# A two-layer FFT-attention kernel: the first element loads its rows in fours and in a fixed order

## The chip, the cores and the metric

The kernel runs on one core of one Trainium2 chip. A core has five engines that run their own instruction queues in order: PE (matrix products), DVE (vector), ACT (activations), POOL and SP. SP, ACT and POOL also issue DMA transfers, which sixteen DMA engines of the core carry out. An instruction starts when the semaphores it waits for have reached their counts. The metric is the device time of one execution in microseconds; the times shown are medians of several executions.

## The reference

The input x is 8 x 256 x 96 x 96 in fp32 (element, channel, row h, column w). Two layers are applied, each on a group-normalised copy and added to x. Cut to what matters here:

```
def _L0_conv_ref(x, w1, b1, w2, b2, w3, b3, w_out, temperature):
    q_f = jnp.fft.fft2(pconv(x, w1, b1), axes=(-2, -1))
    k_f = jnp.fft.fft2(pconv(x, w2, b2), axes=(-2, -1))
    v_f = jnp.fft.fft2(pconv(x, w3, b3), axes=(-2, -1))
    ...
    attn = jnp.einsum('bhcn,bhdn->bhcd', q_f, k_f) * temperature[None].astype(q_f.dtype)
    attn = jax.lax.complex(jax.nn.softmax(jnp.real(attn), axis=-1), jax.nn.softmax(jnp.imag(attn), axis=-1))
    out = jnp.einsum('bhcd,bhdn->bhcn', attn, v_f)
    out = jnp.abs(jnp.fft.ifft2(out, axes=(-2, -1)))
    out = out.reshape(b, c, h, w)
    return pconv(out, w_out)
```

The result is x + L0(gn(x)), and to that is added L1 of its group norm, a linear attention with softplus features; the change doesn't touch L1.

The kernel never forms q_f and k_f. Their products over all frequencies follow from the channel covariance of x with itself and with x mirrored in both axes, so layer 0 begins with sums over pairs (row h from the front, row h from the back, columns reversed).

## The kernel before

Elements are handled one after another, b = 0 to 7, and two SBUF arenas of 128 partitions x 2 planes x 9232 fp32 change roles: `x_of(b)` and `y_of(b)`. For each element there are these stages.

**Pair sums** (`pair_sums`, L335). Twelve blocks u of four row pairs each, and one block for the middle row (u = 12). Rows are loaded by `load_grouped(b, v)` (L136): for v = 0 to 5 it fetches 8 rows f from the front and their 8 mirror rows g from the back, two rows per partition: partition 32a + i holds rows 2(4v + a) and the next, of channels i, i + 32 and so on. Each of the four blocks a has one transfer for f (L152) and one for g (L154), on SP, 32 partitions x 8 runs of 768 bytes, 192 KB. They go to `staged` (plane v % 2). `turn_blocks(u)` (L350) turns 32 x 32 blocks on DVE (L369) from `staged` into `turned`, f into plane 0 and g into plane 1. After the second block of a v, SP writes `turned` to DRAM (`xtd`, L372, 1536 KB), then the next group is loaded. `pair(u)` (L376) forms the sum f + g on POOL (L391) and the difference on DVE (L392) in a ring of five tiles, and `products` puts 24 matmul passes per block on PE (L343), in three steps q.

**Rotation** (`rotate`, L599). 49 steps, each eight matmul passes with a piece of a rotation table R: L647 multiplies rows read back from `xtd` (`fetch`, L633, into seven slots) with R (`load_r`, L608, from the DRAM tensor `rx`), and DVE and ACT move the product to the y arena (L653, L654). R is made at the start by `tables` (L252): a small table is written to DRAM (L266), read back in overlapping form (L270, 1764 KB in runs of 384 bytes) and written out as `rx` (L279, L280). Then follow small loads of weights on ACT (`load_small`).

**Attention** (`attention`), woven with the remaining rotation steps, then **images** (z and po products, L710, L718) and **layer 1**. In images of element b the rows of b + 1 are loaded, and its pair sums run beside images and layer 1. Only element 0 has its pair sums and its rotation alone.

The order on each engine is the order in which the program is written within `manual_schedule` (L1015). For element 0 a loop over the yields of `pair_sums(0)` adds one part of `tables` per turn from the fifth on, a `fetch` every second turn past 20, and a rotation step per turn past 26. The first loads, `gavg` and `gmat` are issued above, outside of `manual_schedule`. Transfers of SP and ACT share eight completion semaphores; before one is used again, its last transfer must have landed.

Of the kernel before, what the change touches and what calls it, by code (L numbers as in the profile page):

```python
# [57 lines left out]
P = 128  # L58
# [4 lines left out]
TR = 4  # L63
# [10 lines left out]
def two_layer_kernel(ctx: ExitStack, tc: tile.TileContext, x, w1t, b1, w2t, b2, w3, b3, wot, temp,  # L74
# [32 lines left out]
    def x_of(b):  # L107
        return arenas[b % 2]
# [15 lines left out]

    SG = NB8 * 2 * W
    TO = 2 * SG + 4

    def staged(b, v, at=0):

        return x_of(b)[:, v % 2, at * SG:at * SG + SG + at]  # L130

    def turned(b):

        return [x_of(b)[:, c, TO:TO + 2 * NQ * C].rearrange("p (q r n) -> p q r n", q=NQ, r=2) for c in range(2)]

    def load_grouped(b, v):  # L136

        xs = x[b].rearrange("(c i) h w -> i c h w", i=32)
        if 2 * v == NG:
            m = H // 2  # L140
            f, g = (staged(b, v, i)[:, 0:C].rearrange("p (c w) -> p c w", c=NB8) for i in range(2))
# [7 lines left out]
        f, g = (staged(b, v, i)[:, 0:SG].rearrange("p (c w) -> p c w", c=NB8) for i in range(2))  # L149
        for a in range(G):  # L150
            h, s = 2 * (G * v + a), slice(32 * a, 32 * a + 32)
            nc.sync.dma_start(out=f[s], in_=xs[:, :, h:h + 2].rearrange("p c r w -> p c (r w)"))  # L152
            if h:
                nc.sync.dma_start(out=g[s], in_=xs[:, :, H - h - 1:H - h + 1].rearrange("p c r w -> p c (r w)"))  # L154
            else:
                nc.sync.dma_start(out=g[s, :, 0:W], in_=xs[:, :, H - 1])
                nc.sync.dma_start(out=g[s, :, W:2 * W], in_=xs[:, :, 0])

    setup = y_of(0)[:, 0, :]
    t0 = setup[0:H, 0:6 * W]  # L160
    nc.scalar.dma_start(out=t0[:, 0:2 * W], in_=tmat[0, :, W:3 * W])
    for v in range(2):
        load_grouped(0, v)


    ident = const.tile([P, P], F32, name="ident")
    make_identity(nc, ident)
# [21 lines left out]
    nc.scalar.dma_start(out=gavg_sb, in_=gavg)  # L189
    gri = setup[:, 6 * W:6 * W + 2 * P]  # L190
    nc.scalar.dma_start(out=gri, in_=gmat)

    pw = const.tile([P, 1], F32, name="pw")
    nc.vector.memset(pw, 1.0)
# [49 lines left out]
    rt = dram.tile([H, 2 * W], F32, name="rt")  # L244
    NP = NG
    RW = TR * (W + 2) + P - W
    rx = dram.tile([NP + 1, W, RW], F32, name="rx")
# [4 lines left out]
    def tables():  # L252

        pcs = ps_tile("pcs")
        for c in range(2):
            nc.tensor.matmul(pcs[0:H, c:c + 1], lhsT=csn[0:1, c, :], rhs=ones[0:1, 0:1], start=True, stop=True)
        cs = t0[:, 5 * W:5 * W + 2]
        nc.vector.tensor_copy(cs, pcs[0:H, 0:2])
        r0 = t0[:, 2 * W:3 * W]
        nc.vector.tensor_scalar_mul(t0[:, 0:W], t0[:, 0:W], cs[:, 0:1])  # L260
        nc.vector.scalar_tensor_tensor(r0, in0=t0[:, W:2 * W], scalar=cs[:, 1:2], in1=t0[:, 0:W], op0=ALU.mult, op1=ALU.add)
        for i in range(2):
            o = (3 + i) * W
# [3 lines left out]
        big = y_of(0)[0:W, 1, 0:(N + 1) * (W + 2) + P - W]  # L267
        rows = big[:, 0:(N + 1) * (W + 2)].rearrange("p (r w) -> p r w", r=N + 1)
        v = rt[0:N + 1, 1:]
        nc.scalar.dma_start(out=rows[:, :, 1:W + 1], in_=bass.AP(v.tensor, v.offset, [[1, W], [2 * W, N + 1], [1, W]]))  # L270
        nc.scalar.copy(rows[:, :, 0:1], csn[0:W, 2, 0:N + 1].unsqueeze(2))
        nc.scalar.mul(rows[:, :, W + 1:W + 2], csn[0:W, 2, 0:N + 1].unsqueeze(2), -1.0)
        nc.scalar.copy(big[:, (N + 1) * (W + 2):], csn[0:W, 2, 0:P - W])
        yield
        for q in range(NQ):
            s = slice(32 * q, 32 * q + 32)
            v = big[s, 0:NP * TR * (W + 2)]
            src = bass.AP(v.tensor, v.offset, [list(v.ap[0]), [TR * (W + 2), NP], [1, RW]])
            nc.scalar.dma_start(out=rx[0:NP].rearrange("i (j q) w -> q j i w", q=NQ)[q], in_=src)  # L279
# [12 lines left out]
        yield from load_small()  # L292
# [42 lines left out]
    def pair_sums(b):  # L335
# [12 lines left out]
        wrap = two.tile([P, 2 * NB8], F32, tag="wrap", name=f"wrap_{b}")  # L348

        def turn_blocks(u):  # L350

            v, r = divmod(u, 2)
            t = turned(b)
            if u == NG:
                f, g = (staged(b, v, i)[0:W, 0:C].rearrange("p (c w) -> p c w", c=NB8) for i in range(2))
# [5 lines left out]
            f = staged(b, v, 0).rearrange("p (c r w) -> p c r w", c=NB8, r=2)  # L361
            if r == 0:
                g = staged(b, v, 1)
                nc.vector.tensor_copy(wrap, g[:, 0:SG:W])
                nc.vector.tensor_copy(g[:, W:SG + 1:W], wrap)
            o = SG + (1 - r) * W + 1
            g = x_of(b)[:, v % 2, o:o + SG].rearrange("p (c n) -> p c n", c=NB8)[:, :, W - 1::-1]
            for i, src in enumerate((f[:, :, r], g)):
                nc.vector.transpose(out=t[i][:, :, r].rearrange("p q (c i) -> p q c i", c=NB8),  # L369
                                    in_=src.rearrange("p c (q w) -> p q c w", q=NQ))  # L370
            if r:
                nc.sync.dma_start(out=xtd[:, v].rearrange("c p m -> p c m"), in_=x_of(b)[:, :, TO:TO + 2 * NQ * C])  # L372
                if v + 2 <= NG // 2:
                    load_grouped(b, v + 2)

        def pair(u):  # L376

            eo = ring_tile(f"eo_{b}_{u}").rearrange("p (q c n) -> p q c n", q=NQ, c=2)
            nq, np_ = (NQ, P) if u < NG else (1, W)
            ft, gt = (t[0:np_, 0:nq, u % 2] for t in turned(b))  # L380
            e, o = (eo[0:np_, 0:nq, c, 1:C + 1] for c in range(2))
            nc.gpsimd.memset(eo[0:np_, 0:nq, :, 0:CB:CB - 1], 1.0 if u < NG else R2)  # L382
            if u == 0:
# [215 lines left out]
    def rotate(b):  # L599
# [5 lines left out]
        def load_r(i):  # L605
            tm = tm_tile(f"tm_{b}_{i}")
            o = (TR if i < NP else 1) * (W + 2) + P - W
            nc.sync.dma_start(out=tm[:, 0:o], in_=rx[i][:, 0:o])  # L608
            return tm

        order = [(c, h, h // TR) for h in range(0, N, 2) for c in range(2)] + [(0, N, NP)]
        area = x_of(b)
        slots = [area[0:W, k, o + 4 * C * i:o + 4 * C * (i + 1)].rearrange("p (c m) -> p c m", c=2)
                 for k, o, n in ((0, LO, 3), (1, LO, 3), (0, LO + 12 * C, 1)) for i in range(n)]
        assert LO + 16 * C <= AW and LO + 12 * C <= LO + NS * CH + 2 * CH
        xts, tms = {}, {}
        at_ = [0]
# [1 line left out]
        def fetch():  # L619
# [36 lines left out]
        def steps():  # L656

            for i in range(len(order)):
                while at_[0] < min(i // 2 + len(slots) - 1, len(order) // 2 + 1):
                    fetch()  # L660
                step(i)
                if i >= 24 and i % 8 == 0 and i // 8 < 6:
                    load_x(b, i // 8 - 3)
                yield

        return fetch, steps()

# [345 lines left out]
    sums = pair_sums(0)  # L1013
    E = mybir.EngineType
    with tc.manual_schedule(engines={E.PE, E.DVE, E.Pool, E.SP, E.Activation}):  # L1015
        parts = tables()
        next(parts)
        fetch, turns = rotate(0)
        for i, _ in enumerate(sums):
            if i > 3:  # L1020
                next(parts, None)
            if i > 20 and i % 2 == 0:
                fetch()
            if i > 26:
                next(turns)
        finish(mix(0, attention(0), turns))
        for b in range(B):
# [60 lines left out]
```

## Time and profile before

| | |
|---|---|
| median of 3 runs | 2663.21 us (2656.18 to 2666.2) |
| time of the profiled execution | 2650.85 us |
| its span (first to last instruction) | 2649.0 us |
| PE busy | 2509.3 us (95%) |
| DVE, ACT, POOL busy | 1789.0, 1155.9, 865.6 us |
| first product of the pair sums (PE L343) | at 16.05 us |
| first rotation step (PE L647) | at 97.11 us |
| last product of the pair sums of element 0 | at 126.46 us, 1.48 us long |
| first z product (PE L710) | at 180.31 us |
| DMA moved | 413.27 MB, mean 156 GB/s |

Busy times are sums over all instructions of an engine. The timeline gives start and length in us; "idle before" names what ended the wait. SPq, ACTq and POOLq are the engines' issue of transfers. DMA share is the mean busy share of the sixteen DMA engines, over 1 where packets overlap.

### The profile page before, as it was taken

To read this page: it belongs to the slowest core of one execution; us is meant where nothing else is said; L and a number is where in the kernel's file an instruction comes from. 1 tells how busy PE (TensorE), PEld (TensorE's weight loads), DVE (VectorE), ACT (ScalarE), POOL (GpSimd) and SP (SyncE) were. 2 spreads that over 40 slices of the span, in tenths; PEclk is the share of its full clock that TensorE was granted. 3 is DMA by queue.
4 is the path that set the end of the run, shared out by engine and by line. 5 is a ranking of instruction groups with operands and counts; after the bars stand their busy time and mean duration, and the time that the engine had idled before them with its cause. 6 is when DMAs were issued, how large, how long until landed. Compare 5 with 4: busy or idle time off the path is not lost. (4 is left out here: it accounts for less than half of the span.)

```text
span 2649.0 us, 41157 instructions
## 1 busy us (share of the span) xinstructions
PE 2509.3 (95%) x15580; PEld 1730.2 (65%) x15580; DVE 1789.0 (68%) x3449; ACT 1155.9 (44%) x1985; POOL 865.6 (33%) x817
## 2 busy tenths in 40 slices
PE   3799999999999999999999999999999999999987
PEld 3775666757677576766668566685666757667544
DVE  3457866577756777568675686757866678766766
ACT  0035353453634526344353544435354353534554
POOL 2213514136042451324422343223523135141311
PEclk8899999999999999999999999999999999999999
DMA  9872628637195461935629264492636826286003
GB/s 210 238 216 60 166 71 270 205 67 189 40 313 161 106 173 57 315 120 143 153 90 305 80 167 129 159 316 42 166 89 230 245 60 179 58 289 210 1 7 144
DMA packets 282797, 413.27 MB, mean 156 GB/s; under 512 B 40772, under 2 KB 208872, under 8 KB 282600
## 3 DMA queue, kind: packets, MB, share of 16 engines
q1 hardware_dynamic: 274304, 406.16, 53.2%
q10 hardware_dynamic: 8296, 4.49, 0.8%
q8 instruction: 123, 2.02, 0.3%
q14 instruction: 74, 0.61, 0.1%
HBM read 256.72 MB, written 153.86 MB: 155 GB/s over the span
## 5 line engine op out<-in xcount | busy, mean ns | idle before, releaser
L710 PE MATMUL z<-arena,mz 128*128 128x384 f32 (+1 forms) x2304 | 593.4, 491 | 0.0
L718 PE MATMUL po<-e,wo 128*128 128x384 f32 x1536 | 527.6, 487 | 1.7 <-ACT e L755 1.7
L754 POOL TENSOR_TENSOR e<-e 128x768 f32<-128x768 f32 x192 | 348.4, 1815 | 552.7 <-ACT e L753 529.3
L343 PE MATMUL acc<-eo 128*128 128x257 f32 (+2 forms) x2368 | 437.1, 336 | 50.0 <-POOL eo L382 23.0
L343 PEld LDWEIGHTS acc<-eo 128*128 128x128 f32 (+1 forms) x2368 | 383.8, 194 | 143.9 <-issue 42.4
L710 PEld LDWEIGHTS z<-arena,mz 128*128 128x128 f32 (+1 forms) x2304 | 310.5, 164 | 236.0 <-issue 51.9
L718 PEld LDWEIGHTS po<-e,wo 128*128 128x128 f32 x1536 | 290.0, 190 | 204.7 <-ACT e L755 7.2
L749 DVE TENSOR_TENSOR e<-z,xT 128x768 f32<-128x768 f32 x384 | 361.9, 950 | 75.4 <-PE z L710 74.9
L647 PEld LDWEIGHTS y<-tm,arena 96*128 96x128 f32 x3072 | 365.9, 195 | 52.9 <-issue 18.9
L647 PE MATMUL y<-tm,arena 96*128 96x128 f32 x3072 | 385.7, 281 | 15.3 <-DMA arena<-xtd 6.4
L753 ACT ACTIVATE e<-e 128x1536 f32<-128x1536 f32 x192 | 284.5, 1482 | 195.2 <-DVE e L749 193.3
L391 POOL TENSOR_TENSOR eo<-arena 128x768 f32<-128x768 f32 x88 | 184.5, 2096 | 536.3 <-DVE arena L369 473.2
L720 DVE TENSOR_TENSOR arena<-arena,po 128x384 f32<-128x384 f32 x384 | 209.9, 553 | 190.0 <-PE po L718 190.0
L755 ACT ACTIVATE e<-e 128x768 f32<-128x768 f32 x192 | 162.0, 844 | 367.1 <-POOL e L754 363.2
L986 POOL TENSOR_TENSOR arena<-arena,po 128x384 f32<-128x384 f32 x180 | 179.1, 1014 | 224.0 <-ACT po L985 224.0
L369 DVE STREAM_TRANSPOSE arena<-arena 128x768 f32<-128x768 f32 x192 | 175.7, 953 | 32.5 <-DMA xtd<-arena 23.0
L299 DVE BATCH_NORM_STATS2 st<-arena 128x6 f32<-128x384 f32 x384 | 194.4, 548 | 0.0
L654 ACT COPY ys<-y 128x4 f32<-128x4 f32 (+1 forms) x200 | 32.4, 162 | 363.8 <-DVE arena L653 363.7
L878 PE MATMUL xT<-ident,arena 128*128 128x128 f32 x1152 | 148.4, 277 | 10.0 <-ACT xT L881 9.6
L878 PEld LDWEIGHTS xT<-ident,arena 128*128 128x128 f32 x1152 | 127.2, 142 | 32.0 <-issue 13.6
L985 ACT COPY po<-o 128x384 f32<-128x384 f32 x180 | 79.0, 485 | 157.4 <-PE o L977 152.4
L653 DVE COPY arena<-y 128x384 f32<-128x384 f32 (+1 forms) x200 | 109.1, 546 | 40.8 <-PE y L647 38.6
(225 smaller groups left out, 2493.1 us busy)
## 6 DMA issues: line engine op xcount, KB each, us to landing
xtd<-arena SPq DMA_DIRECT2D x48, 1536.0 KB
arena<-xtd SPq DMA_DIRECT2D x192, 384.0 KB
arena<-in_x_dram SPq DMA_DIRECT2D x96, 768.0 KB
out_dram<-arena SPq DMA_DIRECT2D x192, 384.0 KB
arena<-in_x_dram SPq DMA_DIRECT2D x376, 192.0 KB
tm<-rx SPq DMA_DIRECT2D x96, 159.0 KB
wl<-in_w1t_dram SPq DMA_DIRECT2D x8, 256.0 KB
wl<-in_w2t_dram SPq DMA_DIRECT2D x8, 256.0 KB
```

Source lines behind the costliest of these rows:

```text
L299: nc.vector.bn_stats(out=st[:, k, c, :], in_=x_of(b)[:, k, c * CH:(c + 1) * CH])
L343: nc.tensor.matmul(acc[c][:, m * (C + 1):m * (C + 1) + C + 1 - m * P], lhsT=eo[0:np_, q, c, 1 + m * P:1 + (m + 1) * P], rhs=eo[0:np_, q, c ...
L391: nc.gpsimd.tensor_add(e, ft, gt)
L647: nc.tensor.matmul(pu[:, o:o + P], lhsT=xt[:, s, k * P:(k + 1) * P], rhs=tm[:, n:n + P], start=True, stop=True)
L710: nc.tensor.matmul(out[:, 0:CH].rearrange("p (h q) -> p h q", q=PR), lhsT=columns(mz, k, c, j), rhs=yz[:, k, f, :, o:o + PR], start=(k == ...
L718: nc.tensor.matmul(po[:, 0:CH], lhsT=wo[:, k, m * P:(m + 1) * P], rhs=e[:, k, :], start=(k == 0), stop=(k == KC - 1))
L720: nc.vector.tensor_add(x[:, m, n], x[:, m, n], po[:, 0:CH])
L749: nc.vector.tensor_add(e[:, 2 * c:2 * c + 2, :].rearrange("p t (q h) -> p t q h", h=H), pz[:, 0:CH].rearrange("p (h q) -> p q h", h=H).uns ...
L753: nc.scalar.activation(e, e, AF.Square)
L754: nc.gpsimd.tensor_add(e[:, 0:2, :], e[:, 0:2, :], e[:, 2:4, :])
L878: nc.tensor.transpose(pt[:, j * C + k * P:j * C + (k + 1) * P], x[:, k, o:o + P], ident)
L986: nc.gpsimd.tensor_add(x[:, m, r], x[:, m, r], t)
```

## The change

Only element 0 and the layout of R in DRAM change.

Rows of element 0 are loaded four to a partition: groups v = 0, 2, 4 of 16 front rows and 16 mirror rows, at 3072 fp32 per half and partition. Groups 0 and 2 lie in the planes of `x_of(0)`, group 4 and the middle row in the y arena. The front half has one transfer per channel group c, eight per group on SP, over 128 partitions, with runs of 1536 bytes; the mirror half stays at one transfer per block of 32 partitions and is issued by ACT. All three groups are issued at the start, inside `manual_schedule`, in program order, with `gavg` and `gmat` behind them on ACT. `turned` gets two places, by v % 2. The writes to `xtd` are issued by POOL. The order of rows in `xtd` changes, and with it the read in `fetch`. R's parts of `tables` come in turns 3 and 9 and from 10 on, `rx` has one long row per partition, rotation steps begin at turn 29 instead of 27, fetches at 18 instead of 22, there are eight slots, and the third `load_x` comes after the steps.

```diff
+    S4 = 2 * SG
+    T4 = 2 * S4 + 4
+    def part_of(b, v, o, n):
+        if b:
+            return x_of(b)[:, v % 2, o:o + n]
+        if 2 * v == NG:
+            return y_of(b)[:, 1, H // 2 * W + H // 4 * HB + o:H // 2 * W + H // 4 * HB + o + n]
+        V = v // 2
+        return x_of(b)[:, V, o:o + n] if V < 2 else y_of(b)[:, 0, 10 * W + o:10 * W + o + n]
+    def turned(b, v):
+        o = TO if b else T4 + v % 2 * 2 * NQ * C
+        return x_of(b)[:, :, o:o + 2 * NQ * C]
...
+        n = 2 if b else 4
+        sg = NB8 * n * W
         for a in range(G):
-            h, s = 2 * (G * v + a), slice(32 * a, 32 * a + 32)
-            nc.sync.dma_start(out=f[s], in_=xs[:, :, h:h + 2].rearrange("p c r w -> p c (r w)"))
+            h, s = 2 * G * v + n * a, slice(32 * a, 32 * a + 32)
+            if b:
+                nc.sync.dma_start(out=f[s], in_=xs[:, :, h:h + n].rearrange("p c r w -> p c (r w)"))
+            else:
+                for c in (2 * a, 2 * a + 1):
+                    z = x[b, 32 * c:32 * c + 32]
+                    nc.sync.dma_start(out=f[:, c], in_=bass.AP(z.tensor, z.offset + 8 * v * W, [[n * W, G], [HW, 32], [1, n * W]]))
+            queue = nc.sync if b else nc.scalar
             if h:
-                nc.sync.dma_start(out=g[s], in_=xs[:, :, H - h - 1:H - h + 1].rearrange("p c r w -> p c (r w)"))
+                queue.dma_start(out=g[s], in_=xs[:, :, H - h - n + 1:H - h + 1].rearrange("p c r w -> p c (r w)"))
...
-    nc.scalar.dma_start(out=t0[:, 0:2 * W], in_=tmat[0, :, W:3 * W])
-    for v in range(2):
-        load_grouped(0, v)
...
-        for q in range(NQ):
-            s = slice(32 * q, 32 * q + 32)
-            v = big[s, 0:NP * TR * (W + 2)]
-            src = bass.AP(v.tensor, v.offset, [list(v.ap[0]), [TR * (W + 2), NP], [1, RW]])
-            nc.scalar.dma_start(out=rx[0:NP].rearrange("i (j q) w -> q j i w", q=NQ)[q], in_=src)
-        nc.scalar.dma_start(out=rx[NP][:, 0:P + 2], in_=big[:, N * (W + 2):N * (W + 2) + P + 2])
+            nc.scalar.dma_start(out=rx.rearrange("(j q) w -> q j w", q=NQ)[q], in_=big[32 * q:32 * q + 32])
+        nc.scalar.dma_start(out=rxm, in_=big[:, N * (W + 2):N * (W + 2) + P + 2])
...
-            if r:
-                nc.sync.dma_start(out=xtd[:, v].rearrange("c p m -> p c m"), in_=x_of(b)[:, :, TO:TO + 2 * NQ * C])
-                if v + 2 <= NG // 2:
+            if u % 2:
+                (nc.sync if b else nc.gpsimd).dma_start(out=xtd[:, v].rearrange("c p m -> p c m"), in_=turned(b, v))
+                if b and v + 2 <= NG // 2 or v + 2 == NG // 2:
                     load_grouped(b, v + 2)
...
-                v, a = divmod(i, G)
+                v, a = divmod(i, G) if b else (i // 8 * 2 + i % 2, i % 8 // 2)
...
     with tc.manual_schedule(engines={E.PE, E.DVE, E.Pool, E.SP, E.Activation}):
+        nc.scalar.dma_start(out=t0[:, 0:2 * W], in_=tmat[0, :, W:3 * W])
+        for v in (0, 2, 4):
+            load_grouped(0, v)
+        nc.scalar.dma_start(out=gavg_sb, in_=gavg)
+        nc.scalar.dma_start(out=gri, in_=gmat)
         parts = tables()
         next(parts)
         fetch, turns = rotate(0)
         for i, _ in enumerate(sums):
-            if i > 3:
+            if i in (3, 9) or i > 9:
                 next(parts, None)
-            if i > 20 and i % 2 == 0:
+            if i > 17 and i % 2 == 0:
                 fetch()
-            if i > 26:
+            if i > 28:
                 next(turns)
```

More of the change, by code (lines that the diff above doesn't have):

```diff
@@ L126, in two_layer_kernel, with blocks_of, middle @@
     TO = 2 * SG + 4
[L128 to L134, printed above, removed]
+    S4 = 2 * SG
+    T4 = 2 * S4 + 4
+    assert T4 + 4 * NQ * C <= AW and NG == 12
+    def part_of(b, v, o, n):
[8 more added lines that the diff above has]
+        return x_of(b)[:, :, o:o + 2 * NQ * C]
+    def blocks_of(b, v):
+        return [turned(b, v)[:, c].rearrange("p (q r n) -> p q r n", q=NQ, r=2) for c in range(2)]
+    def middle(b):
+        return [part_of(b, NG // 2, i * (C + 4), C).rearrange("p (c w) -> p c w", c=NB8) for i in range(2)]
     def load_grouped(b, v):
@@ L140, in load_grouped @@
             m = H // 2
-            f, g = (staged(b, v, i)[:, 0:C].rearrange("p (c w) -> p c w", c=NB8) for i in range(2))
+            f, g = middle(b)
             for q in range(NQ):
@@ L148, in load_grouped @@
             return
-        f, g = (staged(b, v, i)[:, 0:SG].rearrange("p (c w) -> p c w", c=NB8) for i in range(2))
+        n = 2 if b else 4
+        sg = NB8 * n * W
+        f, g = (part_of(b, v, i * sg, sg).rearrange("p (c w) -> p c w", c=NB8) for i in range(2))
         for a in range(G):
-            h, s = 2 * (G * v + a), slice(32 * a, 32 * a + 32)
-            nc.sync.dma_start(out=f[s], in_=xs[:, :, h:h + 2].rearrange("p c r w -> p c (r w)"))
+            h, s = 2 * G * v + n * a, slice(32 * a, 32 * a + 32)
[6 more added lines that the diff above has]
+            queue = nc.sync if b else nc.scalar
             if h:
-                nc.sync.dma_start(out=g[s], in_=xs[:, :, H - h - 1:H - h + 1].rearrange("p c r w -> p c (r w)"))
+                queue.dma_start(out=g[s], in_=xs[:, :, H - h - n + 1:H - h + 1].rearrange("p c r w -> p c (r w)"))
             else:
-                nc.sync.dma_start(out=g[s, :, 0:W], in_=xs[:, :, H - 1])
-                nc.sync.dma_start(out=g[s, :, W:2 * W], in_=xs[:, :, 0])
+                queue.dma_start(out=g[s, :, 0:(n - 1) * W], in_=xs[:, :, H - n + 1:H].rearrange("p c r w -> p c (r w)"))
+                queue.dma_start(out=g[s, :, (n - 1) * W:n * W], in_=xs[:, :, 0])
     setup = y_of(0)[:, 0, :]
     t0 = setup[0:H, 0:6 * W]
-    nc.scalar.dma_start(out=t0[:, 0:2 * W], in_=tmat[0, :, W:3 * W])
-    for v in range(2):
-        load_grouped(0, v)
     ident = const.tile([P, P], F32, name="ident")
@@ L188, in two_layer_kernel @@
     gavg_sb = const.tile([P, P], F32, name="gavg_sb")
-    nc.scalar.dma_start(out=gavg_sb, in_=gavg)
     gri = setup[:, 6 * W:6 * W + 2 * P]
-    nc.scalar.dma_start(out=gri, in_=gmat)
     pw = const.tile([P, 1], F32, name="pw")
@@ L246, in two_layer_kernel @@
     RW = TR * (W + 2) + P - W
-    rx = dram.tile([NP + 1, W, RW], F32, name="rx")
+    RL = (N + 1) * (W + 2) + P - W
+    rx = dram.tile([W, RL], F32, name="rx")
+    rxm = dram.tile([W, P + 2], F32, name="rxm")
     xtd = dram.tile([2, NG // 2, P, 2 * NQ * C], F32, name="xtd")
@@ L266, in tables @@
         nc.scalar.dma_start(out=rt, in_=t0[:, 3 * W:5 * W])
-        big = y_of(0)[0:W, 1, 0:(N + 1) * (W + 2) + P - W]
+        yield
+        big = y_of(0)[0:W, 1, 0:RL]
         rows = big[:, 0:(N + 1) * (W + 2)].rearrange("p (r w) -> p r w", r=N + 1)
@@ L346, in products @@
                                      skip_group_check=True)
-        wrap = two.tile([P, 2 * NB8], F32, tag="wrap", name=f"wrap_{b}")
+        n = 2 if b else 4
+        sg = NB8 * n * W
+        wrap = two.tile([P, n * NB8], F32, tag=f"wrap{n}", name=f"wrap_{b}")
         def turn_blocks(u):
-            v, r = divmod(u, 2)
-            t = turned(b)
+            v, r = u // 2, u % n
+            t = blocks_of(b, v)
             if u == NG:
-                f, g = (staged(b, v, i)[0:W, 0:C].rearrange("p (c w) -> p c w", c=NB8) for i in range(2))
+                f, g = (m[0:W] for m in middle(b))
                 nc.vector.tensor_copy(g[0:32, :, 31:32], f[0:32, :, 0:1])
@@ L360, in turn_blocks @@
                 return
-            f = staged(b, v, 0).rearrange("p (c r w) -> p c r w", c=NB8, r=2)
+            f = part_of(b, v, 0, sg).rearrange("p (c r w) -> p c r w", c=NB8, r=n)
             if r == 0:
[L363 to L367, printed above, removed]
+                nc.vector.tensor_copy(wrap, part_of(b, v, sg, sg)[:, ::W])
+                nc.vector.tensor_copy(part_of(b, v, sg + W, sg - W + 1)[:, ::W], wrap)
+            g = part_of(b, v, sg + (n - 1 - r) * W + 1, sg).rearrange("p (c n) -> p c n", c=NB8)[:, :, W - 1::-1]
             for i, src in enumerate((f[:, :, r], g)):
-                nc.vector.transpose(out=t[i][:, :, r].rearrange("p q (c i) -> p q c i", c=NB8),
+                nc.vector.transpose(out=t[i][:, :, u % 2].rearrange("p q (c i) -> p q c i", c=NB8),
                                     in_=src.rearrange("p c (q w) -> p q c w", q=NQ))
-            if r:
-                nc.sync.dma_start(out=xtd[:, v].rearrange("c p m -> p c m"), in_=x_of(b)[:, :, TO:TO + 2 * NQ * C])
-                if v + 2 <= NG // 2:
+            if u % 2:
+                (nc.sync if b else nc.gpsimd).dma_start(out=xtd[:, v].rearrange("c p m -> p c m"), in_=turned(b, v))
+                if b and v + 2 <= NG // 2 or v + 2 == NG // 2:
                     load_grouped(b, v + 2)
@@ L379, in pair @@
             nq, np_ = (NQ, P) if u < NG else (1, W)
-            ft, gt = (t[0:np_, 0:nq, u % 2] for t in turned(b))
+            ft, gt = (t[0:np_, 0:nq, u % 2] for t in blocks_of(b, u // 2))
             e, o = (eo[0:np_, 0:nq, c, 1:C + 1] for c in range(2))
@@ L607, in load_r @@
             o = (TR if i < NP else 1) * (W + 2) + P - W
-            nc.sync.dma_start(out=tm[:, 0:o], in_=rx[i][:, 0:o])
+            nc.sync.dma_start(out=tm[:, 0:o], in_=rx[:, i * TR * (W + 2):i * TR * (W + 2) + o] if i < NP else rxm)
             return tm
@@ L612, in rotate @@
         area = x_of(b)
+        places = ((0, LO, 3), (1, LO, 3), (0, LO + 12 * C, 1)) if b else ((0, T4 - 16 * C, 4), (1, T4 - 16 * C, 4))
         slots = [area[0:W, k, o + 4 * C * i:o + 4 * C * (i + 1)].rearrange("p (c m) -> p c m", c=2)
-                 for k, o, n in ((0, LO, 3), (1, LO, 3), (0, LO + 12 * C, 1)) for i in range(n)]
+                 for k, o, n in places for i in range(n)]
         assert LO + 16 * C <= AW and LO + 12 * C <= LO + NS * CH + 2 * CH
@@ L661, in steps @@
                 step(i)
-                if i >= 24 and i % 8 == 0 and i // 8 < 6:
+                if i >= 24 and i % 8 == 0 and i // 8 < 6 and (b or i < 40):
                     load_x(b, i // 8 - 3)
                 yield
+            if b == 0:
+                load_x(b, 2)
         return fetch, steps()
```

## The prediction

> **What bounds the kernel now.** I read the page's busy times first, then stretches of 20 us, PE's own timeline of the first 130 us, the waits there, and last the moves around one write to `xtd`.
>
> ```profile
> PE 2509.3 (95%) x15580; PEld 1730.2 (65%) x15580; DVE 1789.0 (68%) x3449; ACT 1155.9 (44%) x1985; POOL 865.6 (33%) x817
> PE   3799999999999999999999999999999999999987
> DMA  9872628637195461935629264492636826286003
> ```
>
> PE is the bound of the whole, except in the first slices, the only ones the change touches. What element 0 gains or loses before its images stage moves everything behind it by as much, since from there on PE is full.
>
> Stretches of 20 us; columns are length, busy PE, PEld, DVE, ACT, POOL with counts, granted clock, DMA share, GB/s:
>
> ```profile
> 0.00:20.00 20.00, 4.75 (x16) 4.14 (x17) 9.77 (x39) 2.05 (x5) 4.24 (x62) 1.00 1.02 191
> 60.00:80.00 20.00, 10.84 (x52) 9.53 (x53) 9.10 (x12) 0.00 (x0) 8.59 (x7) 0.76 0.97 215
> 140.00:160.00 20.00, 20.00 (x146) 17.76 (x146) 10.60 (x25) 6.05 (x18) 2.05 (x4) 1.00 1.00 271
> ```
>
> PE is half idle up to 110 us and full from 120 on. Its own timeline, in start and length:
>
> ```profile
> 16.05 10.49 PE L343 MATMUL acc<-eo 128*128 128x257 f32 x48 [11.65 <-DVE eo L388]
> 36.73 10.40 PE L343 MATMUL acc<-eo 128*128 128x257 f32 x48 [10.20 <-POOL eo L391]
> 62.26 9.60 PE L343 MATMUL acc<-eo 128*128 128x257 f32 x48 [15.12 <-POOL eo L382]
> 78.76 9.88 PE L343 MATMUL acc<-eo 128*128 128x257 f32 x48 [6.90 <-POOL eo L382]
> 126.46 1.48 PE L343 MATMUL acc<-eo 96*128 96x257 f32 x8
> ```
>
> The rows x48 are two blocks u each; between them it waits for POOL's sums, 10 to 15 us a time. The last product ends at 126.46 + 1.48 = 127.9 us. That is the mark I carry over.
>
> Waits up to 130 us (total, times, longest), and the timeline around one write:
>
> ```profile
> POOL eo L391 <- DVE arena L369: 81.3, 10, 20.6
> DVE wrap L364 <- DMA arena<-in_x_dram: 20.9, 5, 6.0
> DVE arena L369 <- DMA xtd<-arena: 20.4, 4, 7.4
> ```
>
> ```profile
> 78.82 0.38 SPq L372 DMA_DIRECT2D xtd<-arena  x1
> 85.00 0.31 SPq L152 DMA_DIRECT2D arena<-in_x_dram  x1
> 85.01 1.84 DVE L369 STREAM_TRANSPOSE arena<-arena 128x768 f32<-128x768 f32 x2 [3.12 <-DMA xtd<-arena]
> ```
>
> POOL waits for DVE's turns, and DVE for two things: rows of x, and the landing of the last `xtd` write, because it must not overwrite `turned`. The write issued at 78.82 frees DVE at 85.01, 6.2 us later; the others took 7.8 (24.26 to 32.10), 5.7 (51.97 to 57.63) and 6.5 (67.66 to 74.14).
>
> [...] The new front loads have the source pattern [[384, 4], [9216, 32], [1, 384]]: its slowest dimension is 4[...]. The trace of before agrees where it can: the four small loads of `bkq4` and `tcol`, whose source also begins with a 4, have four completion increments each in its completion records, those of x and of `rt`'s read-back sixteen, those of `wo` over 8 partitions eight. No large transfer on four engines is in it. [...] No POOL-issued transfer is in the trace of before.
>
> **The change part by part.** A: *rows of four, front half.* Stores of 1536-byte runs give the price of such a packet:
>
> ```profile
> 2630.00:2640.00 10.00, 9.25 (x51) 5.81 (x48) 9.68 (x21) 3.13 (x7) 6.09 (x7) 1.00 1.05 387
> ```
>
> 387 GB/s at 1.05 packets on each of 16 engines is 1536 x 16 x 1.05/387 = 67 ns. A front transfer has 128 packets; on four engines 32 each, 2.13 us; on sixteen it would be 0.53. Taken without the overlap the price is 63.5 ns (2.6 us less at the second group in B); few engines may not overlap as well, and I keep 67. A mirror transfer, 256 packets on sixteen engines, is 1.07 us. The 24 front transfers alone [...]draw 92 GB/s, where before drew 235 (6 to 9 us).
>
> B: *fixed order on eight shared semaphores.* In the built program the third mirror transfer of the first group waits for SP's 15th front transfer, the fourth for the 18th, the second group's four for the 19th to 22nd. So no group is complete before most front rows are in. [...] The 18th has landed at 1.9 + 18 x 2.13 + 3 x 1.07 + 1 = 44.5; with 3 us for the fourth mirror, the first group is complete at 47.5. The second: 1.9 + 22 x 2.13 + 7 x 1.07 + 1 + 3 = 60.3. Before, the first pair of rows was there at 11.77.
>
> C: *PE's start.* wrap 0.4, two turns 1.84, three vector operations 2.9 (11.77 to 16.05 before): 47.5 + 5.2 = 52.7 instead of 16.05. Two blocks could not run through then: POOL's first `xtd` write also waits for the second group's mirrors, since the region of `turned` as tracked, from plane 0 to plane 1, spans it, and behind it on POOL stands the sum of u = 1. So it is issued at 60.3.
>
> D: *two places for `turned`.* They remove less than they look to: in the built program DVE's turn of u = 2, 6, 10 still waits for the previous write to land, that of u = 4, 8 with its second half. The write from POOL I take as 7.7 us: 6.2 as measured[...].
>
> E: *the chain of writes.* Per pair of blocks: turn 1.84, difference 0.96, turn 1.84, write 7.7; 0.9 less for v = 2 and 4; 3.4 more after u = 4 (the `gsel` copies, 36.67 to 40.13 before); 0.8 more for the first write beside mirrors. Writes land at 68.8, 81.1, 96.0, 108.4, 119.9. Turn and sum of u = 10: 1.9 + 2.6, so PE has it at 124.4 (u = 9 with two rotation steps is done before). Then per block 3 x 1.48 + 3 x 1.06 = 7.6 us (rows from 113 us on): u = 11 ends at 139.6, u = 12 at 141.1. Against 127.9 that is +13.2.
>
> F: *steps moved.* Eight instead of ten rotation steps stand before the last product: 2 x 1.06 = +2.1 behind it, where PE is full.
>
> G: *R later.* On ACT `rt` stands behind all mirrors, at about 63; read-back to 78 (19 us before among x loads, from 9.2), `rx` to 87, then 28 small loads, 14 us before, between which SP's fetches take turns: first pieces by 90 to 100. The first step needs them at about 118. Hidden; with less than 18 us of slip it costs nothing, beyond that each us. `gmat`, at about 58, is hidden likewise (needed at 83). The fifth and sixth fetch hold POOL's last write (they wait for the write landing at 119.9), and SP's seventh fetch waits for that one: about 132, needed at step 12, past 141.
>
> H: *slots, `load_x`, `rx` rows*: the eighth slot only helps; the third `load_x` is needed by the fifth `po` block; `rx` pieces keep their 1696-byte runs. Nothing; if the third `load_x` came late, some us.
>
> Sum: +13.2 + 2.1 = +15.3. The profiled execution took 2650.85, so 2666.2; the runs shown have a median 12.4 us above it, 2663.21, so 2678.5 us.
>
> **Rivals.** *Sixteen engines after all*[...]: packets of 67 ns then let 4.6 MB (18 front and 3 mirror transfers) in by 17 us, group 1 by 29, and the write chain starts 31 us earlier: 110.3 for the last product, 2663.2 - 17.6 + 2.1 = 2648. That is the other side: it holds if the first write is issued before 60.3 - 15.3 = 45 us. Against it: the four increments of the small loads. *POOL's writes are dear*: each us over 7.7 counts five times; at 10 us +11.5, 2690. [...] *R takes over*: slip of 30 instead of 18 us gives +12, 2690. For it: ACT's queue is in order and every small load waits for one eight uses back; against: the margin. *The new buffers do nothing*: that is, the chain E doesn't bind and PE, once fed, runs through. u = 1 then starts at 63 (first POOL write at 60.3 and the sum's 2.6), and 11.3 blocks of 4.9 us (9.6 to 10.4 for two) and eight steps end at 127: 2663.2 - 0.9 + 2.1 = 2664, no change. For it: two places should free DVE; against it: the waits in the built program.
>
> **How the numbers follow.** 0.5% is 13.3 us, about what can be told from no change. Four engines with the sum as above: 0.72, 2665 to 2692, of it 0.42 slower and 0.30 same. POOL or R dearer: 0.15, 2688 to 2710, slower. Sixteen engines: 0.08, 2637 to 2658, 0.05 faster, 0.03 same. Writes off the path: 0.05, same. So slower 0.57, same 0.38, faster 0.05. 2652 to 2702 leaves out about 2 in 10.
>
> **What would show it.** Right: GB/s near 90 to 130 in the first 40 us, first PE L343 between 46 and 60, POOLq's first `xtd` issue some 8 us later, then DVE L369 waiting on `xtd` five times, last product at 135 to 148. Wrong: a first product near 25 us[...], packets well off 67 ns, PE waiting on `tm` for long at its first L647, writes far off 7.7.

## The result, and the profile after

The changed kernel takes 2684.14 us (median of 4 runs, 2679.74 to 2688.84), the kernel before 2659.69 us beside it (4 runs, 2647.57 to 2666.2). The ratio is 1.0105, 95% interval 1.008 to 1.013 (the quotient of these two medians is 1.009): slower by about 1%. The forecast was 2678.5 us, a loss of 15.3 us. The two medians lie 24.5 us apart, the profiled executions, 2650.85 and 2679.74 us, 28.9 us. Sign and place were right, the size was about half of what came.

From the page of the changed kernel, the busy times and PE's and the DMA engines' tenths in 40 slices:

```profile
PE 2509.0 (94%) x15580; PEld 1733.1 (65%) x15580; DVE 1791.1 (67%) x3443; ACT 1155.3 (43%) x1985; POOL 872.6 (33%) x823
PE   1699999999999999999999999999999999999988
DMA  4872644916377262954619365491646926286003
```

PE's work is the same to 0.3 us; the first slice fell from 3 to 1 and the second from 7 to 6, and the DMA engines are half idle in the first. From the first z product to the end the changed kernel takes 2678.0 - 211.82 = 2466.2 us, the kernel before 2649.0 - 180.31 = 2468.7 at nearly the same granted clock. So the loss lies wholly ahead of the first z product, where it is 31.5 us.

Stretches of the changed kernel (length, busy PE, PEld, DVE, ACT, POOL with counts, granted clock, DMA share, GB/s):

```profile
0.00:20.00 20.00, 0.80 (x4) 0.71 (x4) 2.08 (x29) 1.57 (x2) 3.07 (x60) 1.00 0.36 110
20.00:30.00 10.00, 0.00 (x0) 0.00 (x0) 0.00 (x0) 0.00 (x0) 0.00 (x0) 1.00 0.27 97
```

Between 20 and 30 us nothing computes at all: the whole core waits for rows that come at 97 GB/s, with a quarter of the DMA engines' time in use. In the first 20 us before it was 191 GB/s at a share of 1.02.

PE's timeline and the waits up to 160 us (total, times, longest):

```profile
58.21 6.61 PE L362 MATMUL acc<-eo 128*128 128x257 f32 x24 [53.77 <-DVE eo L407]
74.01 5.58 PE L362 MATMUL acc<-eo 128*128 128x257 f32 x24 [9.19 <-POOL eo L401]
85.45 10.60 PE L362 MATMUL acc<-eo 128*128 128x257 f32 x48 [5.87 <-POOL eo L410]
156.18 1.48 PE L362 MATMUL acc<-eo 96*128 96x257 f32 x8
```

```profile
DVE wrap L384 <- DMA arena<-in_x_dram: 48.1, 1, 48.1
POOL eo L410 <- DVE arena L388: 34.9, 5, 8.9
DVE arena L388 <- DMA xtd<-arena: 29.6, 5, 8.6
```

The first product starts at 58.21 instead of 16.05. DVE waits 48.1 us for the first rows, once, where it waited 20.9 us in five pieces before. Its waits for the landing of a write to `xtd` have not gone: five instead of four, 29.6 us instead of 20.4, in spite of the two places for `turned`. The last product ends at 157.66, before at 127.94: +29.7 us, and the first z product follows 31.5 us later than before. Of the 42 us that PE starts late, 12 are made up on the way.

### The profile page after: what moved, and what is told of

The parts are those of the page before. It is cut to its first block, busy times and chain, and to the rows that moved or that the text cites. A ratio compares the mean times of both kernels' runs of the same rounds, so it can differ in the third digit from the quotient of the medians.

```text
span 2678.0 us, 41124 instructions
## 1 busy us (share of the span) xinstructions
PE 2509.0 (94%) x15580; PEld 1733.1 (65%) x15580; DVE 1791.1 (67%) x3443; ACT 1155.3 (43%) x1985; POOL 872.6 (33%) x823
## 5 line engine op out<-in xcount | busy, mean ns | idle before, releaser
L900 PEld LDWEIGHTS xT<-ident,arena 128*128 128x128 f32 x1152 | 127.4, 142 | 31.4 <-issue 13.6
```

What stands on the lines that cost most here:

```text
L900: nc.tensor.transpose(pt[:, j * C + k * P:j * C + (k + 1) * P], x[:, k, o:o + P], ident)
```

## The experiments

Behind the first z product all kernels do the same work, and what they take there varies from 2461 (clock 0.987) to 2480 us (0.975), for the most part with the granted clock. So beside the ratio to the kernel before (95% interval) the table gives, from each timeline in us, the start of the first product, the issue of the first write to `xtd`, and the end of the last product of element 0's pair sums, which the clock hardly touches. The expectations also name profiled times; those carry the 18 us of spread behind the first z product, so I judge by the last product.

| kernel | first product | first write | last product ends | ratio |
|---|---|---|---|---|
| before | 16.05 | 24.26 | 127.94 | 1 |
| after | 58.21 | 70.22 | 157.66 | 1.0105 (1.008 to 1.013) |
| e1 front half by rows | 22.39 | 31.24 | 119.51 | 0.9981 (0.9961 to 1.0001) |
| e2 before, front half by channel group | 24.34 | 44.26 | 158.61 | 1.0113 (1.0083 to 1.0144) |
| e3 writes by SP | 57.98 | 67.54 | 154.72 | 1.0114 (1.0068 to 1.016) |
| e4 writes split by plane | 57.45 | 59.55 | 141.91 | 1.0069 (1.0043 to 1.0096) |
| e8 before, writes by POOL | 16.28 | 26.30 | 134.00 | 1.0022 (1.0004 to 1.0039) |
| e9 mirrors on SP | 39.06 | 73.56 | 157.35 | 1.0133 (1.0086 to 1.0181) |
| e10 mirrors on SP, R late | 36.65 | 58.57 | 156.96 | 1.0109 (1.007 to 1.0147) |
| e13 no read-back | 57.80 | 69.20 | 156.35 | 1.0127 (1.0095 to 1.0159) |
| e5 e1 and e4 together | 23.03 | 25.13 | 110.46 | 0.9935 (0.9915 to 0.9956) |
| e7 and R early | 21.89 | 23.99 | 103.44 | 0.9919 (0.9895 to 0.9943) |
| e11 read-back after the third group | 22.42 | 24.52 | 107.37 | 0.9925 (0.9897 to 0.9953) |
| e14 third mirrors on SP | 21.81 | 23.91 | 105.85 | 0.9939 (0.9916 to 0.9962) |

The theory: the front transfers run on four engines, the rows come late, and the chain of turn and write behind them passes that on. The rivals: the writes by POOL or the order of the queues cost the time, or R.

**The front half alone.** e1 is the changed kernel without the channel groups:

```diff
-            if b:
-                nc.sync.dma_start(out=f[s], in_=xs[:, :, h:h + n].rearrange("p c r w -> p c (r w)"))
-            else:
-                for c in (2 * a, 2 * a + 1):
-                    z = x[b, 32 * c:32 * c + 32]
-                    nc.sync.dma_start(out=f[:, c], in_=bass.AP(z.tensor, z.offset + 8 * v * W, [[n * W, G], [HW, 32], [1, n * W]]))
+            nc.sync.dma_start(out=f[s], in_=xs[:, :, h:h + n].rearrange("p c r w -> p c (r w)"))
```

> The changed kernel, with only the front half of element 0 loaded as the mirror half is: per group four transfers over 32 partitions each, instead of eight by channel group over 128. The packets stay 1536 bytes. Theory (front transfers run on four engines, and the late first rows set everything behind them): the stretch of 0 to 20 us draws over 250 GB/s instead of 110, the first product moves from 58 us to 15-25 us, the first write to xtd from 70 us to 20-27 us, and since 87 us lay between that write and the last product, the last product comes at 105-118 us instead of 158: 2632 to 2642 us profiled, below the kernel before. Rival (the writes by POOL and the fixed order cost the time, not the loads): the first product moves little or the gain is eaten by the chain of writes, 2660 us or more.

A stretch of it, and its timeline:

```profile
0.00:20.00 20.00, 0.79 (x4) 0.71 (x4) 3.88 (x33) 1.56 (x2) 3.07 (x60) 1.00 0.99 218
```

```profile
22.39 7.20 PE L357 MATMUL acc<-eo 128*128 128x257 f32 x24 [17.96 <-DVE eo L402]
31.24 0.95 POOL L386 DMA_DIRECT2D xtd<-arena  x1 [27.60 <-DMA arena<-in_x_dram]
118.03 1.48 PE L357 MATMUL acc<-eo 96*128 96x257 f32 x8
```

The same bytes in the same runs of 1536 bytes now draw 218 GB/s at a share of 0.99, instead of 110 at 0.36. The first write comes 39.0 us earlier and the last product 38.2: what the rows gain reaches the end undiminished. The mechanism held, the numbers were too good (218 GB/s where over 250 were expected, the first write 4 us later, since it waits for the second group, the last product 1.5 us outside), and the ratio is only at the edge of a gain.

Four engines or sixteen, the completion records show by the sign that the prediction read in the small loads. In the changed kernel each front transfer has four completion increments when it lands, in e1 each has sixteen. And from 23 to 37 us, when in the changed kernel they are alone, the packet records show four to six packets under way at any time, 4.3 in the mean (a DMA share of 0.27 of sixteen engines), and the front transfers land one after another, 2.03 us apart: 32 packets of 65 to 67 ns, the medians there, are 2.1 us. The records name no engine; that each increment stands for one is read from this agreement.

e2 puts that one part into the kernel before:

```diff
-            nc.sync.dma_start(out=f[s], in_=xs[:, :, h:h + 2].rearrange("p c r w -> p c (r w)"))
+            if b:
+                nc.sync.dma_start(out=f[s], in_=xs[:, :, h:h + 2].rearrange("p c r w -> p c (r w)"))
+            else:
+                for c in (2 * a, 2 * a + 1):
+                    z = x[b, 32 * c:32 * c + 32]
+                    nc.sync.dma_start(out=f[:, c], in_=bass.AP(z.tensor, z.offset + 8 * v * W, [[2 * W, G], [HW, 32], [1, 2 * W]]))
```

> The kernel before, with only the front half of element 0 loaded by channel group over 128 partitions: eight transfers of 128 packets of 768 bytes per group in place of four of 256; nothing else of the change. Theory (four engines): a front transfer takes 32 packets of 36 ns on one engine, 1.15 us, so a group 9.2 + 2.3 us instead of 4.6; the first product comes at 18-22 us instead of 16, and each later group, already waited for (20.9 us in five waits), comes some 3 to 7 us later: 15 to 30 us slower than before, ratio 1.005 to 1.011. Rival (number of engines is not it, a load by channel group costs what a load by rows costs): ratio 0.998 to 1.002.

The last product comes 30.7 us later than before, about as much as in the whole change (29.7). (The 36 ns expected for a packet of 768 bytes is the median of the kernel before between 52 and 55 us.) But not all of it is the four engines. In its timeline SP stands still (start, length):

```profile
11.00 0.34 ACTq L275 DMA_DIRECT2D arena<-rt  x1
14.62 16.32 SPq L157 DMA_DIRECT2D arena<-in_x_dram  x2
44.30 0.17 DVE L369 COPY wrap<-arena 128x16 f32<-128x16 f32 x1 [16.24 <-DMA arena<-in_x_dram]
```

The second of these two transfers waits for a shared semaphore whose last user is R's read-back, issued at 11.00 and landed about 19 us later; the profile puts 15.1 us of SP's time down to that one wait. More transfers per group (eight and four instead of four and four) shifted which transfer takes which semaphore. The direct cost was near the expectation: the first group came at 20.05 instead of 11.77, 8.3 us later where 6.9 were reckoned, and the first product at 24.34, outside the 18 to 22 expected. The 15 us of standing behind R were not expected at all, so the ratio, at the upper end of what was expected, agrees in part by luck.

**The chain of writes.** e4 leaves the loads as they are and makes each write to `xtd` as two:

```diff
-                (nc.sync if b else nc.gpsimd).dma_start(out=xtd[:, v].rearrange("c p m -> p c m"), in_=turned(b, v))
+                if b:
+                    nc.sync.dma_start(out=xtd[:, v].rearrange("c p m -> p c m"), in_=turned(b, v))
+                else:
+                    for c in range(2):
+                        nc.gpsimd.dma_start(out=xtd[c, v], in_=turned(b, v)[:, c])
```

> The changed kernel, with each write to xtd of element 0 made as two, one per plane, still by POOL. In the built program the first write then no longer waits for the second group's mirrors, and DVE's turn of a pair of blocks waits for the write of two pairs earlier, not for the last one: the two places of turned do what they were laid out for. The front loads stay on four engines. Theory (late rows, and behind them a chain of write and turn that doesn't allow to catch up): first product still at 54-60 us; POOL's first write at about 61 instead of 70; then PE takes the blocks at 4.9 us each, the last product at 125-138 us instead of 158, 2648 to 2660 us profiled, about as before. Rival (PE, DVE or R bind after the late start and the writes are beside the path): 2672 to 2682.

```profile
59.55 1.40 POOL L395 DMA_DIRECT2D xtd<-arena  x2 [55.92 <-DVE arena L388]
63.82 16.03 PE L362 MATMUL acc<-eo 128*128 128x257 f32 x96 [0.18 <-POOL eo L405]
88.62 20.44 PE L362 MATMUL acc<-eo 128*128 128x257 f32 x112 [8.77 <-POOL eo L405]
122.63 2.04 PE L671 MATMUL y<-tm,arena 96*128 96x128 f32 x8 [13.57 <-issue]
```

The first write goes out right behind the turn, 10.7 us earlier, and PE then takes up to 112 passes in one piece (x96, x112) where it took 24 or 48. None of DVE's waits for `xtd` is left among the waits up to 160 us. The last product ends 15.8 us earlier, at 141.91 where 125 to 138 were expected, for two other waits came into the open: DVE waits 7.7 us for `gmat` and PE 8.8 us behind it, and PE stands 13.6 us before its first rotation step, for R. So the chain did bind, and R stands next in line; the rival was right in part. (The profiled time, 2678.1 us, lies in the rival's range, but behind the first z product this execution takes 12.4 us longer than that of the changed kernel, at a clock of 0.979 instead of 0.985.)

e3 and e8 ask for the price of POOL as the writer. e3 is the changed kernel with `nc.sync` at that line, e8 the kernel before with `nc.gpsimd` there for b = 0.

> The changed kernel, with the writes of element 0 to xtd issued by SP, as before, instead of POOL. Theory (five writes of 9.0 us from issue to the next turn stand in a chain, against 6.5 for SP's before[...]): the mean comes down to 6-8 us and the last product from 158 to 145-153 us: 2667 to 2675 us profiled. Rival (who issues makes no difference, the writes are slowed by the loads beside them): mean stays 8.5 to 10, 2677 to 2683. A loss is possible as well: writes on SP then stand behind the fetches of R, which wait for it until about 100 us; then the fourth and fifth write are late, and it is 2680 to 2695.

> The kernel before, with the writes of element 0 to xtd issued by POOL instead of SP, nothing else: the disputed price by itself. Theory of the prediction (7.7 us from issue to the next turn instead of 6.5 us on average, four times on the path): +5 us; if the 9.0 us that the changed kernel showed is POOL's own doing, +10 us, ratio 1.002 to 1.004. Rival (it was the loads beside the writes): mean of 6 to 7 us as before and no difference, ratio 0.998 to 1.001. In the run with SP's writes in the changed kernel the mean was 7.9 us, which lies between.

From issue to DVE's next turn the five writes took 10.6, 9.3, 10.5, 7.4 and 7.0 us by POOL (after), and 9.2, 11.0, 8.9, 5.3 and 5.3 by SP (e3): means of 9.0 and 7.9. In the last two POOL's writes are 1.9 us longer; the first three are slow whoever writes. The last product gains 2.9 us, less than expected.

In e8 the last product comes 6.1 us later than before, ratio 1.0022, near the 5 us expected, and the four writes that DVE waits for take 6.8, 10.3, 5.7 and 7.0 us, a mean of 7.4 against 6.5. But the loss did not come by the path of that sum: DVE waits 14.3 us in all for landings, where it waited 20.4 before. What is new is that POOL stands 10.6 and 8.3 us ahead of two of its writes, for rows of x, and the sum of the next block stands behind each in POOL's order. So the 6.1 us are the price of the write and of its place on POOL together, and e8 does not separate the two.

**The order.** e9 puts `queue = nc.sync` for the mirrors, so that each stands on SP behind the front transfers of its partitions; e10 in addition sends R's rows (`next(parts)`) in turn 1 of the loop instead of ahead of it.

> The changed kernel, with the mirror transfers of element 0 on SP's queue, each behind the front transfers of its 32 partitions, instead of on ACT's; the front transfers stay by channel group. Theory (beside the four engines it is the fixed order that makes the first group late: its last mirrors wait on a shared semaphore for the 15th and 18th front transfer): now the first group is complete after its own 8 front and 4 mirror transfers, 8 x 2.13 + 4 x 1.07 + 3 = 24 us instead of 54, the second at about 46 instead of 70; first product 27-33 us, first write 45-50 us, last product 130-138 us instead of 158, 2650 to 2660 us profiled. Rival (only the four engines count, whatever the order): the first product stays over 45 us and the last over 148. Gain by R, which is no longer behind the mirrors, is not expected to show: it was in time.

> The changed kernel with the mirrors of element 0 on SP behind the front transfers of their 32 partitions, as in the run before, but R's rows go out only after the first block, so that no load of x on SP waits for a semaphore of R's transfers (there SP stood 17 us behind the read-back, and the second group came no earlier). Theory (the fixed order over shared semaphores makes the first two groups late, on top of the four engines): first product 30-40 us instead of 58, the second group and the first write at 46-56 us instead of 70, the last product at 134-146 us instead of 158. Rival[...]: first write at 60 us or later, last product over 148.

e9's timeline, a run of two front transfers on SP:

```profile
12.31 0.34 ACTq L292 DMA_DIRECT2D arena<-rt  x1
22.61 17.29 SPq L176 DMA_DIRECT2D arena<-in_x_dram  x2
```

The first product comes at 39.06 instead of 58.21, so the order did cost the first group some 19 us. But the second group came at 73.5: SP stood until 39.9, again at a semaphore that R's read-back had taken (15.1 us). That spoiled the test, and the rival's number for the last product came out for another reason. The rival of e10 was that the front transfers, 24 of 2.13 us or 51 us in all by estimate, hold the second group back in any order. Without that stop, in e10, the first product and the first write came 21.6 and 11.7 us earlier than in the changed kernel, the first product within the theory's range, the first write between the two. Yet the last product ended at 156.96, 0.7 us earlier and on the rival's side. Its five writes took 10.4, 13.2, 12.0, 9.8 and 9.2 us, a mean of 10.9 against 9.0. The first stood beside front transfers still on their way (SP issues the last at about 72 us); what slowed the later ones is not settled.

e13 takes away a suspect, the read-back of R:

```diff
-        nc.scalar.dma_start(out=rows[:, :, 1:W + 1], in_=bass.AP(v.tensor, v.offset, [[1, W], [2 * W, N + 1], [1, W]]))
+        nc.scalar.copy(rows[:, :, 1:W + 1], csn[0:W, 2, 0:N + 1].unsqueeze(2).to_broadcast([W, N + 1, W]))
```

> The changed kernel without the read-back of R from rt: ACT fills the rows of R with a constant from a table instead, so that the images are wrong; all else is as it was, the pieces written to rx too. It asks why the first three writes to xtd took 10.6, 9.3 and 10.5 us and the last two 7.4 and 7.0. Theory (the excess is the traffic of R, moved beside them): rx goes out at about 76 us, beside the first write, which stays at 9 to 11 us, and the second and third come down to 6.5-8.5 us; last product at 151-155 us instead of 158. Rival (the loads of x[...] make it): the three stay at 9 to 11 us, last product 156-159.

The writes took 12.5, 7.8, 8.6, 8.7 and 6.9 us: the second and third came down by 1.5 and 1.9, the first, now beside `rx`, and the fourth went up. The mean, 8.9, and the last product, 156.35, hardly moved; the rival's number for the end. R's transfers are one neighbour among several, and not the one that sets the end.

**Both remedies.** e5 is e1 and e4 together; e7 sends R's rows behind the first group and reads them back behind the second (`load_grouped(0, 0)`, `next(parts)`, `load_grouped(0, 2)`, `next(parts)`, `load_grouped(0, 4)`), and its further parts follow from turn 4 on; e11 moves that read-back behind the third; e14 is e7 with the third group's mirrors on SP.

> The changed kernel with both remedies: front half in four transfers per group over 32 partitions, and each write to xtd made as two, one per plane, by POOL. Theory: rows early as in the first (first product 22 us), writes out of the chain as in the fourth, so that R binds next: in the run with the split writes 70 us lay from the issue of rt to the last product; with rt at 35 us the last product comes at 103-108 us instead of 119.5: 2625 to 2635 us profiled. Rival (the chain of writes no longer matters when the rows are early): 117-121 us, 2640 to 2646.

> As the kernel with both remedies, and R earlier: its rows go out after the first group's mirrors, its read-back after the second's, its other pieces from the fifth block on. Theory (R binds once writes and rows do not): the wait of PE before its first rotation step goes, the blocks run at about 4.9 us each from 22 us on, with 3 us for the gsel copies and eight steps of 1.06 us, and the last product comes at 92-100 us: 2615 to 2628 us profiled, the best of all. Rival (R's read-back among the loads of x delays rows and R alike, as in the kernel before): 103 us or more, no gain over the kernel with both remedies.

> The kernel with both remedies and R early, with the read-back of R behind the third group's mirrors instead of ahead of them on ACT, where they waited (12.5 us of DVE's wait for the third group, 10.2 us of PE's at 71 us). Theory (the queue order holds the third group): the third group comes before 50 us, PE runs through, last product at 90-98 us instead of 103: ratio 0.987 to 0.991 to the kernel before. Rival (R then is late instead, and PE waits for it before its first rotation step): last product 100-108, ratio 0.991 to 0.994, no better than the last.

> The kernel with both remedies and R early (read-back ahead of the third group on ACT), with the third group's mirrors on SP, behind that group's front transfers, so that they no longer stand behind the read-back. Theory (in the two runs with R early, either the third group or R was late, because they stood in one queue): the third group comes before 55 us and R's first pieces by 72, PE waits for neither over 5 us, last product at 90-98 us instead of 103, ratio 0.986 to 0.991. Rival (the loads share the engines, so what one gains the other loses): last product 101-107, ratio 0.991 to 0.994.

The last product ends at 110.46 with both, against 119.51 with the rows alone: the theory's side, 2.5 us short of it. With R early (e7) it ends at 103.44, a gain of 7.0 us more, but above the 92 to 100 expected and just at the rival's figure. PE of e7:

```profile
21.89 15.33 PE L357 MATMUL acc<-eo 128*128 128x257 f32 x76 [17.46 <-DVE eo L406]
39.93 20.99 PE L357 MATMUL acc<-eo 128*128 128x257 f32 x116 [2.72 <-DVE eo L410]
71.09 8.74 PE L357 MATMUL acc<-eo 128*128 128x257 f32 x40 [10.17 <-POOL eo L409]
```

The 10.17 us are the third group, whose mirrors stood behind the read-back. Moving one ahead of the other did not help: in e11 the third group is in time, and PE waits 19.1 us before the first rotation step; in e14 the last mirror of the third group waits for the read-back's semaphore, and the read-back itself takes 38 us (25.81 to 63.85). Both ended on the rival's side. The ratios of e7, e11 and e14 cannot be told apart; these three and e5 are faster than the kernel before, e7 by 0.6 to 1.05%.

## Why the prediction was right, and where it was not

**A, front transfers on four engines: right.** The third mirror of the first group, which waits for the 15th front transfer, went out at 37.35; the step's arithmetic gives 1.9 + 15 x 2.13 + 2 x 1.07 + 1 = 37.0, where 1.9 is an estimate of the transfers' start from the 86 GB/s of the first 3 us before. The completion increments, four in the changed kernel and sixteen in e1, the 4.3 packets under way, and the 97 GB/s at a share of 0.27 against e1's 218 at 0.99 agree with that. Which four engines they were, and whether every front transfer had the same ones, no record names; that they landed 2.03 us apart speaks for the same ones. The number of engines was not varied with all else equal, for e1 also has half as many front transfers, of twice the size; so what the four engines alone cost at the end is known less exactly than that there were four.

**B, the order: right in the waits, wrong in a size.** The mirrors that complete the first and the second group, and the first write:

```profile
45.27 0.32 ACTq L179 DMA_DIRECT2D arena<-in_x_dram  x1
60.22 0.82 ACTq L179 DMA_DIRECT2D arena<-in_x_dram  x2
70.22 0.95 POOL L391 DMA_DIRECT2D xtd<-arena  x1 [66.58 <-issue]
```

They went out at 45.27 (44.5 counted) and 60.22 (57.3 counted; the x2 holds the third group's first mirror too). The step gave a mirror 3 us to land, an estimate; by the completion records these two took 8.5 and 9.0 us. Of the first one's sixteen increments twelve came by 50.1 and the last four at 53.5 to 53.7; of the second's, twelve by 64.3 and the last four at 68.8 to 69.2. Four is also the number of a front transfer's increments, so the late share is probably the one that stood on the four engines of the front transfers; the records name no engine, so this is not shown. The front transfers gave way in turn: the last of their increments came 2.03 us apart up to 39.4, and from the 19th to the 22nd 4.3 us apart (47.15 to 60.19), where the step counts 2.13 and 1.07 for a mirror. The packet records show medians of 137 to 153 ns per packet of 1536 bytes between 48 and 52 us and of 142 to 145 between 64 and 68, in place of 65. This put the first product 5.5 us behind its forecast of 52.7 and the first write 9.9 us behind 60.3, the largest of the misses: 2.9 in the issue of the last mirror, 6.0 in its landing, 1.0 from there to the write.

**C, D, the waits that stay: right.** The first write and the sum of u = 1 were held for the second group's mirrors, and DVE waited five times for `xtd`. That these waits come from the region of both planes as tracked, and not from a lack of places, e4 shows: with a write per plane they are gone. Of POOL's price of 7.7 us, 6.2 was the length of one of SP's writes; the other 1.5 was an estimate with no measurement behind it. e8 gives 7.4 in the mean, by single writes of 5.7 to 10.3. In the changed kernel the mean was 9.0, the first three being slow with SP as well.

**E, the sum: what was mis-sized.** The chain of writes, at its end:

```profile
136.56 1.84 DVE L388 STREAM_TRANSPOSE arena<-arena 128x768 f32<-128x768 f32 x2 [5.16 <-DMA xtd<-arena]
```

The last product ended 16.6 us later than forecast (157.66 against 141.1): 9.9 by the first write, which is B's mirror, 2.1 by that write's own length (10.6 us for 8.5), 4.6 by the four periods of the chain behind it (80.83 to 136.56, 55.7 us for 51.1). From the fifth landing to the end it was 21.1 us, 21.2 forecast. The step took the writes' length from the kernel before, and put them where the loads of three groups, R's transfers and the small loads are crowded into the first 125 us. Which of these neighbours sets the length is open: e13 takes one away and e10 moves some, and the mean does not fall (8.9 and 10.9).

That the time came as near as it did is in part luck. The profiled execution was 13.5 us above the forecast for it (2679.74 for 2666.2), the median only 5.6, because the forecast was added to the median of three runs, 2663.21, and with the fourth the median before is 2659.69. The last product, looked for at 135 to 148 us, missed its sign; the first product between 46 and 60 and the five waits for `xtd` met theirs. (One reading of the part on what bounds the kernel is loose: of the waits between PE's pieces one is 6.9 us, not 10 to 15. No sum rests on it.)

**F: right.** The gap to the kernel before grew from 29.7 at the last product to 31.5 at the first z product, 1.8 us for the 2.1 of two steps; in e2, which leaves the steps where they were, it stays at 30.7.

**G: right, with an edge.** R's first piece went out at 101.22 (90 to 100 forecast) and the first step began at 135.90, without a wait. e4 and e11, where PE is sooner, stand for it 13.6 and 19.1 us.

**H: nothing seen**, the rest of the kernel being 2.5 us shorter than before at a clock 0.001 higher.

Of the rivals, sixteen engines and R did not come, and the chain of writes did bind; the dear writes came in part. Taken apart by e1, the front half by channel group cost 38.2 us at the last product (after less e1), and all else of the change gained 8.4 (e1 against before).

## What to carry to other kernels

When a load is laid over all partitions at once, look at the slowest dimension of its pattern, for here the number of completion increments went with it: four where it was 4 (the front transfers, `bkq4`, `tcol`), sixteen where it was 32 (the mirrors, e1's front transfers), and 110 GB/s against 218 in the first 20 us. Such a load seems to hold up others beside it as well: the mirrors' last four increments came 3.6 and 4.9 us behind their twelfth. A buffer doubled to remove a wait does so only if the region that a transfer is seen to touch is as small as the transfer: one write per plane took the wait away, two places did not. Price a moved transfer with its new neighbours, and where queues share a few semaphores, look up whose landing each issue waits for: in e2 and e9 SP stood 15 us behind R's read-back, with which its loads have nothing to do.

## What the runs showed of the hardware

The read-back of R, 1764 KB in runs of 384 bytes, took 12.2 us in the changed kernel (78.96 to 91.12), 19.2 before, 15.9 in e1, and 34.2 and 38.0 in e7 and e14, where it lay among loads of x and writes.

A small DVE copy is slow beside POOL's sum. From the timeline of the changed kernel:

```profile
53.91 0.19 DVE L384 COPY wrap<-arena 128x32 f32<-128x32 f32 x1 [48.14 <-DMA arena<-in_x_dram]
86.74 2.58 POOL L410 TENSOR_TENSOR eo<-arena 128x768 f32<-128x768 f32 x1
87.56 1.85 DVE L384 COPY wrap<-arena 128x32 f32<-128x32 f32 x1
```

The same instruction takes 0.19 us alone and 1.85 us where a sum is under way on POOL, and it ends at 89.41, 0.09 us after the sum (89.32). At 119.86, beside the sum of 119.04 to 121.62, it takes 1.84 us, and in e8, at 28.29, beside the sum of 27.47 to 30.04, 1.82; in the kernel before, where it didn't meet a sum, 0.17 to 0.18. DVE's turns are not slowed: two at 83.65 take 1.83 us beside a sum (82.81 to 85.40), and two at 54.31, with no sum on POOL, 1.84. What holds the copy the trace doesn't name. The wait at 87.56 costs nothing, for DVE then waits until 95.09 for the write anyway; without that wait it would cost 1.7 us, an estimate from these two durations.
